# Query products of two heads as a seven-product block scheme in a two-layer decoder kernel

## The chip, the cores and the metric

The kernel runs on one core of a Trainium2 chip. The metric is the device time of one execution in microseconds (us). The kernel before took 1770.25 us, the median of three runs (1769.23 to 1772.86). Engines are named as the profile names them: PE is TensorE's matmul row and PEld its weight loads, DVE is VectorE, ACT is ScalarE, POOL is GpSimd, SP is SyncE, whose queue issues most DMAs.

## What is computed

Two decoder layers with layernorm after each of four blocks, on 4 x 256 tokens of width 512, all in float32. The change lies in the first block, a latent attention with 32 heads:

```
q_c = x @ Wq_c.T + bq_c                     # 192 wide
q   = q_c @ Wq_up.T + bq_up                 # per head 128 + 64 (rotary part)
kv  = x @ Wkv_c.T + bkv_c                   # 64 latent + 64 rotary
k   = [kv_nope @ Wk_up.T + bk_up, kv_rope]  # per head 128 + 64
v   = kv_nope @ Wv_up.T + bv_up
out = softmax(q k^T / sqrt(192)) v  ->  summed through Wo;   x = layernorm(x + out)
```

After it come a gated FFN with integer weights (1376 inner columns), a causal attention with 32 heads of 128, and a linear layer with eight low-rank experts, each followed by its layernorm.

## The kernel before, in words

**Setup (lines 101 to 189).** The weights of the first block are loaded by DMA. The key up-projection is folded into the query up-projection: for each head, a matrix `wm` of 128 + 1 columns maps the 192 + 1 compressed query rows (two pieces of 96 rows, the second with a row of ones for the bias) straight to a 128-wide query against the latent key `kT`. The 64 folded columns are computed in eight groups of four heads from `wqn` and `wkn` (line 64, copied by lines 184); the 64 rotary columns come by DMA (lines 140 to 142). `wm` is stored with the head index innermost, so one head's matrix is read with a step of 32 elements. `qcT` holds the compressed queries of all 1024 tokens, in the two pieces.

**Folded queries (lines 191 to 206).** `q_unit(h, hf)` makes the query of one head for one half of the tokens (512): two matmuls, one per piece, added up in a PSUM bank "p", then one ScalarE copy with the softmax scale. A pair of heads takes four units, eight products of 512 columns. The first pair's are made before the loop; in the loop each of the four batch steps of pair j makes one unit of pair j + 1.

**The loop (lines 297 to 318).** Sixteen head pairs j, and in each four batch steps b. A step computes the scores of its two heads (`scores0`, two banks "s"), takes row maxima on VectorE, forms the exponent's bias with `beta`, and lets ScalarE take the four exponentials with row sums. Meanwhile PE transposes the probabilities of the step before (`transposes0`, line 265, banks "t"); VectorE copies each bank to SBUF as `pT` (line 269); one query unit follows; then the output products of the step before with the latent values `cN` (`output0`, line 282, bank "o"), copied by ScalarE into `pc` (line 286). VectorE divides the new probabilities by their sums (`softmax0`, line 254). Every second pair, `value_unit` multiplies `pc` of two pairs with the value weights into `oacc` (lines 288 to 295).

**After the loop (lines 320 to 324).** For each of eight token tiles: product with `wo`, residual add (line 323), layernorm, four transposes of the new x (line 98), copy to `xT` (line 99). Then the FFN begins with the last, narrow weight chunk (`last_chunk`, line 386 on: gate in "p", up in "s"), for each token half, and with the input differences of its own seven-product scheme (line 360).

**What sets the order.** The code calls the engines in the order of the loops; the tile framework reorders each engine's instructions by its own estimate of times, and puts in the waits. PSUM has eight banks of 128 x 512 words: in this stage two each for "p", "s", "t" and "o", kept in one pool (`ps0`) that stays open through the FFN and closes behind it.

Of the kernel before, what the change touches and what calls it, by code (L numbers as in the profile page):

```python
# [9 lines left out]
F32 = mybir.dt.float32  # L10
I32 = mybir.dt.int32
AF = mybir.ActivationFunctionType
ALU = mybir.AluOpType
# [3 lines left out]
P = 128  # L17
B, S, D = 4, 256, 512
N = B * S
NT = N // P  # L20
DC = D // P
NH = 32
GH = 4
NG = NH // GH
DN, DR, DV = 128, 64, 128
RQ, RKV = 192, 64
RQ2 = RQ // 2
# [8 lines left out]
QSCALE = 1.0 / math.sqrt(DN + DR)  # L36
# [3 lines left out]
def tile_decoder2(ctx: ExitStack, tc: tile.TileContext, a: dict, out: bass.AP):  # L40
    nc = tc.nc
# [5 lines left out]
    @contextmanager  # L47
    def banks(name, **bufs):

        with tc.tile_pool(name=name, bufs=1, space=PSUM) as pool:  # L50
            ps["pool"], ps["bufs"] = pool, bufs
            yield

    def bank(tag, shape=(P, 512)):
        return ps["pool"].tile(list(shape), F32, tag=tag, name=f"ps_{tag}", bufs=ps["bufs"][tag])
# [6 lines left out]
    def mm(o, pairs):  # L62
        for i, (l, r) in enumerate(pairs):
            nc.tensor.matmul(o, l, r, start=(i == 0), stop=(i == len(pairs) - 1))  # L64
# [40 lines left out]
    NP = NH // 2  # L105
    FP = 2
    ps0 = ExitStack()
    ps0.enter_context(banks("ps0", p=2, s=2, t=2, o=2))
    with tc.tile_pool(name="l0", bufs=1) as l0, tc.tile_pool(name="l0b", bufs=2) as l0b:
        wkn = l0.tile([P, NH, RKV + 1], F32, name="wkn")  # L110

        wm = l0.tile([RQ2 + 1, 2, P + 1, NH], F32, name="wm")
# [7 lines left out]
        qcT = l0.tile([RQ2 + 1, 2, N], F32, name="qcT")  # L120
# [9 lines left out]
        for c in range(DC):  # L130
            nc.scalar.dma_start(out=wqc[:, c, :], in_=a["wqc"][:, c, :])
            nc.scalar.dma_start(out=wkvc[:, c, :], in_=a["wkvc"][:, c, :])
            for hf in range(2):
                cols = bass.ts(hf, 512)
# [16 lines left out]

        nc.vector.memset(qcT[RQ2:RQ2 + 1, 1, :], 1.0)
        outs = []
        for hf, tags in enumerate(("pst", "pst")):
            for m in range(3):
                rows_m = P if m == 2 else RQ2
                outs.append((bank(tags[m]), hf, m, rows_m))
        for c in range(DC):  # L160
            for pj, hf, m, rows_m in outs:
                lhs = wkvc[:, c, :] if m == 2 else wqc[:, c, m * RQ2:(m + 1) * RQ2]
# [3 lines left out]
        for pj, hf, m, rows_m in outs:  # L166
            cols = bass.ts(hf, 512)
# [3 lines left out]
                nc.vector.tensor_scalar(qcT[:RQ2, m, cols], pj[:RQ2], cb[:RQ2, m:m + 1], None, ALU.add)  # L171


        for g in range(NG):
            heads = slice(g * GH, (g + 1) * GH)
            for m in range(2):
                rows_m = RQ2 + m
                pj = bank("o", (P, GH, RKV + 1))
                for hh in range(GH):
                    mm(pj[:rows_m, hh, :], [  # L180
                        (wqns[g][:, hh, m * RQ2:m * RQ2 + rows_m], wkn[:, g * GH + hh, :])
                    ])
                copy = nc.scalar.copy if m == 0 else nc.vector.tensor_copy
                copy(wm[:rows_m, m, DR:, heads], pj[:rows_m].rearrange("p h c -> p c h"))

            tp = bank("t", (P, P))
            nc.tensor.transpose(tp, kT[:, bass.ts(g, P)], ident)
            nc.vector.tensor_copy(cN[:, g, :], tp[:, DR:])

        qh = {}  # L190

        def q_unit(h, hf):

            if h not in qh:
                qh[h] = l0b.tile([P, N], F32, tag=f"qh{h % 2}", name=f"qh{h}")
            cols = bass.ts(hf, 512)
            pj = bank("p")
            mm(pj, [
                (wm[:RQ2, 0, :P, h], qcT[:RQ2, 0, cols]),
                (wm[:, 1, :P, h], qcT[:, 1, cols]),  # L200
            ])
            nc.scalar.activation(qh[h][:, cols], pj, AF.Copy, scale=QSCALE)

        for u in [(h, hf) for h in range(2) for hf in range(2)]:
            q_unit(*u)

        beta = l0.tile([P, NT, NH], F32, name="beta")
        for t in range(NT):
            toks = bass.ts(t, P)
            pj = bank("p", (P, NH))  # L210
            mm(pj, [
                (qcT[:RQ2, 0, toks], wm[:RQ2, 0, P, :]),
                (qcT[:, 1, toks], wm[:, 1, P, :]),
            ])
            nc.scalar.activation(beta[:, t, :], pj, AF.Copy, scale=QSCALE)

        bvs = bv[:, 0:1]
        for n in (16, 8, 4, 2, 1):
# [3 lines left out]
        def scores0(j, b):  # L222
            keys = bass.ts(b, S)
            scs = []
            for h in (2 * j, 2 * j + 1):
                sc = bank("s", (P, 2, S))
                for qt in range(2):
                    mm(sc[:, qt, :], [(qh[h][:, bass.ts(2 * b + qt, P)], kT[:, keys])])
                scs.append(sc)
            nmx = small.tile([P, 2, 2], F32, name="nmx")  # L230
            for i, sc in enumerate(scs):
                nc.vector.tensor_reduce(nmx[:, i, :], sc, AX.X, ALU.max, negate=True)  # L232

            be = beta[:, 2 * b:2 * b + 2, 2 * j:2 * j + 2].rearrange("p t h -> p h t")
            nmb = small.tile([P, 2, 2], F32, name="nmb")
            nc.vector.tensor_tensor(nmb, nmx, be, ALU.subtract)
            bias = small.tile([P, 2, 2], F32, name="ebias")
            nc.vector.tensor_tensor(bias, nmb, be, ALU.add)  # L238
            pr = l0b.tile([P, 2, 2, S], F32, tag="pr", name="pr")
            sm = small.tile([P, 2, 2], F32, name="sm")  # L240
            for i, sc in enumerate(scs):
                for qt in range(2):
                    nc.scalar.activation(  # L243
                        pr[:, i, qt, :], sc[:, qt, :], AF.Exp, bias=bias[:, i, qt:qt + 1],
                        accum_out=sm[:, i, qt:qt + 1],
                    )
            return pr, sm
# [11 lines left out]
        def transposes0(pr):  # L259
            pTs = []  # L260
            for i in range(2):
                tp = bank("t", (P, 2, S))
                for kt in range(2):
                    for qt in range(2):
                        nc.tensor.transpose(  # L265
                            tp[:, kt, qt * P:(qt + 1) * P], pr[:, i, qt, kt * P:(kt + 1) * P], ident
                        )
                pT = l0b.tile([P, 2, S], F32, tag=f"pT{i}", name=f"pT{i}")
                nc.vector.tensor_copy(pT, tp)  # L269
                pTs.append(pT)  # L270
            return pTs

# [14 lines left out]

        def value_unit(j0, hf):
            cols = bass.ts(hf, 512)
            pj = bank("p")  # L290
            mm(pj, [(wvl[:, j, :], pc[j][:, cols]) for j in range(j0, j0 + FP)])
            if j0 == 0:
                nc.vector.tensor_scalar(oacc[:, cols], pj, bvs, None, ALU.add)
            else:
                nc.vector.tensor_tensor(oacc[:, cols], pj, oacc[:, cols], ALU.add)

        pending, flush = None, []
        for j in range(NP):
            if j == 1:
                for t in range(NT):  # L300
                    nc.gpsimd.tensor_tensor(x[:, t, :], x[:, t, :], bo, ALU.add)
            todo = [(h, hf) for h in (2 * j + 2, 2 * j + 3) for hf in range(2)] if j + 1 < NP else []
            for b in range(B):
                pr, sm = scores0(j, b)
                if pending:
                    pTs = transposes0(pending[2])
                if todo:
                    q_unit(*todo.pop(0))
                if flush and b >= 2:
                    value_unit(*flush.pop(0))  # L310
                if pending:
                    output0(pending[0], pending[1], pTs)
                pending = (j, b, softmax0(pr, sm))
            if j % FP == FP - 1:
                flush += [(j + 1 - FP, hf) for hf in range(2)]
# [2 lines left out]
            value_unit(*u)  # L318

        for t in range(NT):  # L320
            pj = bank("p")
            mm(pj, [(oacc[:, t * P:(t + 1) * P], wo0)])
            nc.vector.tensor_tensor(x[:, t, :], pj, x[:, t, :], ALU.add)
            layernorm(t)
# [14 lines left out]


    Q = 2 * P
    with tc.tile_pool(name="f0", bufs=1) as f0:
        dsc = f0.tile([P, D], F32, name="dsc")
        nc.sync.dma_start(out=dsc, in_=a["rows"][:, 1, :])
        hT = f0.tile([P, NI, N], F32, name="hT")
# [16 lines left out]
        with tc.tile_pool(name="f0i", bufs=2) as f0i, tc.tile_pool(name="f0w", bufs=3) as f0w:  # L362
# [82 lines left out]
            for c in range(NI2):  # L445
# [5 lines left out]
                for hf in range(2):  # L451
                    quarters = [slice((2 * hf + m) * Q, (2 * hf + m + 1) * Q) for m in range(2)]
                    cols = bass.ts(hf, 512)
                    up = f0w.tile([P, 2, 512], F32, tag="up", name="up", bufs=1)
                    products(lg, rights[hf], [[hT[:, 2 * c + n, q] for q in quarters] for n in range(2)])
                    for n in range(2):
                        h = hT[:, 2 * c + n, cols]
                        nc.scalar.activation(h, h, AF.Silu, scale=gsc[:, 2 * c + n:2 * c + n + 1])
                    products(lu, rights[hf], [[up[:, n, m * Q:(m + 1) * Q] for m in range(2)] for n in range(2)])
                    for n in range(2):  # L460
                        h = hT[:, 2 * c + n, cols]
# [16 lines left out]
        with tc.tile_pool(name="f0d", bufs=2) as f0d:  # L478
# [59 lines left out]
            for tt in range(NT // 2):  # L538
# [3 lines left out]
                down(tt, *now)  # L542
                for m in range(2):
                    layernorm(2 * tt + m)

    ps0.close()

# [4 lines left out]
    with banks("ps1", b0=1, b1=1, b2=1, s=2, t=2, o=1), \  # L554
# [4 lines left out]
        def xblock(k, m):  # L559
            return xT[:, 2 * k:2 * k + 2, m * HN:(m + 1) * HN]  # L560
# [6 lines left out]
        t3 = xcomb("t3", xblock(1, 1), xblock(0, 1))  # L567
        t1 = xblock(0, 1)
        nc.vector.tensor_tensor(t1, t1, xblock(0, 0), ALU.subtract)
        t2 = xcomb("t2", xblock(1, 1), t1)  # L570
        t4 = xcomb("t4", xblock(1, 0), t2)
# [214 lines left out]
        for j in range(NP):  # L786
# [15 lines left out]
            total, at, todo = sum(w for _, w in order), 0, {}  # L802
# [4 lines left out]
            for i in range(2 * B):  # L807
                h, b = 2 * j + i // B, i % B
# [5 lines left out]
                if pending:  # L814
                    pT = transposes1(pending[2])
# [18 lines left out]
    with banks("ps2", p=2, s=2, t=2, o=2), tc.tile_pool(name="f1", bufs=2) as f1:  # L834
        iscale = 1.0 / math.sqrt(DK)
        for t in range(NT):
            cols = bass.ts(t, P)
# [24 lines left out]
            tp = bank("t", (P, P))  # L862
# [91 lines left out]
```

## Time and profile before

| what | us |
|---|---|
| median of the runs | 1770.25 |
| the profiled execution | 1776.69 |
| its span | 1774.9 |
| set-up to the first folded queries | 0 to 39.0 |
| first pair's queries, beta, first scores | 39.0 to 54 |
| head-pair loop | 54 to 436 |
| residual, layernorm, first FFN matmuls | 436 to 472 |
| the rest | 472 to 1774.9 |

In the profile a group line reads: line of the kernel, engine, operation, output<-input by tile name, shapes, count | busy us, mean ns of one | idle time of the engine just before, and what ended most of it. A timeline line reads: start us, length us, engine, line, operation, and in brackets the idle time before it. An f32 matmul appears as two PE instructions, and its recorded length overlaps that of the next; what it costs is the distance from its start to the next start. A stretch line gives its bounds, its span, the busy us of PE, PEld, DVE, ACT and POOL with counts, the granted PE clock, the DMA share and GB/s.

### The profile page before, as it was taken

The numbers are of one execution on the slowest core, as the hardware profiler recorded it, in microseconds if no ns is written. First come the engines' busy times: TensorE is split into PE (matmuls) and PEld (weight loads), VectorE is DVE, ScalarE is ACT, GpSimd is POOL, SyncE is SP. The second block draws the span as 40 slices with busy tenths as digits, with TensorE's granted clock in tenths as the row PEclk, the third lists the DMA queues.
The fourth block names the chain that finished last, engine by engine and source line by source line (L and its number), as shares of the span: only waits on it lengthen the run. The fifth ranks groups of instructions, "written<-read, shape, count | busy, mean of one in ns | idle before, by whom it ended". The sixth has DMA issues, their size and how long they took to land.

```text
span 1774.9 us, 20762 instructions
## 1 busy us (share of the span) xinstructions
PE 1728.0 (97%) x7376; PEld 1206.1 (68%) x7376; DVE 1079.4 (61%) x2556; ACT 480.7 (27%) x1570; POOL 493.8 (28%) x516
## 2 busy tenths in 40 slices
PE   8999999999899998999999999999999999999988
PEld 5666666665588884767667767766776776676644
DVE  1677777767745544456656566666656665567844
ACT  1444444443222100222222222222222222222223
POOL 0200000000457335122434244234325334333220
PEclk9999999999999999999999999999999999999989
DMA  8000000000521000101001011001011010010000
GB/s 277 1 1 1 1 1 1 1 1 1 185 72 36 1 1 20 40 24 48 24 24 48 25 36 48 24 24 48 25 43 42 24 48 24 19 47 25 12 12 36
DMA packets 30985, 60.85 MB, mean 34 GB/s; under 512 B 2689, under 2 KB 20353, under 8 KB 29153
## 3 DMA queue, kind: packets, MB, share of 16 engines
q1 hardware_dynamic: 29474, 58.86, 10.6%
q8 instruction: 59, 0.97, 0.2%
q10 hardware_dynamic: 1408, 0.66, 0.1%
q14 instruction: 44, 0.36, 0.1%
HBM read 57.41 MB, written 2.10 MB: 34 GB/s over the span
## 4 chain that ended last, share of the span: by engine, by line
PE 88%; DVE 7%; DMA 2%; issue 1%; ACT 1%; POOL 1%; ACTq 0%; DVEq 0%; POOLq 0%
PE ps_b L629 20%; PE ps_s L64 12%; PE ps_b L653 11%; PE ps_p L64 10%; PE ps_b L700 9%; PE ps_o L282 4%; PE ps_t L265 3%; PE ps_o L779 3%; PE ps_s L419 3%; PE ps_t L768 2%; PE ps_o L64 2%; PE ps_o L419 2%; PE ps_p L419 2%; PE ps_o L780 2%; DVE pr L762 1%
## 5 line engine op out<-in xcount | busy, mean ns | idle before, releaser
L781 ACT COPY att<-ps_o 128x256 f32<-128x256 f32 x128 | 47.6, 372 | 521.6 <-PE ps_o L780 521.5
L243 ACT ACTIVATE pr<-ps_s,ebias 128x256 f32<-128x256 f32 x256 | 117.7, 472 | 203.0 <-DVE ebias L238 203.0
L708 DVE TENSOR_TENSOR x<-ps_b,x 128x512 f32<-128x512 f32 x180 | 122.9, 685 | 39.6 <-PE ps_b L700 29.0
L718 POOL TENSOR_TENSOR x<-x,po 128x512 f32<-128x512 f32 x90 | 112.3, 1268 | 123.4 <-DVE x L708 95.0
L752 ACT ACTIVATE pr<-ps_s,nmx 128x128 f32<-128x128 f32 (+1 forms) x256 | 105.4, 418 | 144.5 <-DVE nmx L748 144.5
L64 PE MATMUL ps_s<-kT,qh 128*128 128x256 f32 x512 | 130.8, 393 | 1.0 <-ACT pr L243 0.6
L64 PE MATMUL ps_p<-qcT,wm 96*128 96x512 f32 (+1 forms) x256 | 126.5, 618 | 0.0
L373 POOL CAST fwg<-wiwg 128x512 f32<-128x512 int32 (+1 forms) x12 | 7.4, 643 | 401.8 <-DMA wiwu<-in_wu 392.7
L762 DVE TENSOR_SCALAR pr<-pr,rc 128x128 f32<-128x128 f32 (+1 forms) x256 | 115.0, 481 | 4.3
L64 PEld LDWEIGHTS ps_s<-kT,qh 128*128 128x128 f32 x512 | 89.9, 189 | 36.3 <-ACT pr L243 20.6
L232 DVE TENSOR_REDUCE nmx<-ps_s 128x2 f32<-128x512 f32 x128 | 88.1, 688 | 37.9 <-PE ps_s L64 35.4
L64 PE MATMUL ps_s<-ck,cq 128*128 128x128 f32 (+1 forms) x512 | 106.1, 329 | 0.0
L744 DVE TENSOR_TENSOR ps_s<-ps_s,mask 128x256 f32<-128x256 f32 x128 | 55.3, 432 | 70.1 <-PE ps_s L64 66.9
L700 PE MATMUL ps_b<-ct,co 128*128 128x256 f32 x360 | 88.9, 381 | 4.0 <-POOL co L680 4.0
L269 DVE COPY pT<-ps_t 128x512 f32<-128x512 f32 x128 | 86.4, 681 | 0.0
L64 PEld LDWEIGHTS ps_p<-qcT,wm 96*128 96x128 f32 (+1 forms) x256 | 70.9, 299 | 17.6
L748 DVE TENSOR_REDUCE nmx<-ps_s 128x1 f32<-128x128 f32 (+1 forms) x256 | 79.5, 352 | 4.3
L779 PE MATMUL ps_o<-pT,v 128*128 128x256 f32 x256 | 77.3, 384 | 4.0 <-DVE pT L770 4.0
L254 DVE TENSOR_SCALAR pr<-pr,rc 128x256 f32<-128x256 f32 x256 | 79.0, 349 | 3.1
L768 PEld LDWEIGHTS ps_t<-ident,pr 128*128 128x128 f32 x384 | 50.1, 141 | 41.5 <-issue 31.6
L700 PEld LDWEIGHTS ps_b<-ct,co 128*128 128x128 f32 x360 | 67.7, 190 | 13.4 <-POOL co L680 4.2
L779 PEld LDWEIGHTS ps_o<-pT,v 128*128 128x128 f32 x256 | 47.9, 191 | 40.4 <-issue 36.5
(244 smaller groups left out, 3580.1 us busy)
## 6 DMA issues: line engine op xcount, KB each, us to landing
w_wa<-in_wq SPq DMA_DIRECT2D x16, 512.0 KB, 3.9
w_wb<-in_wk SPq DMA_DIRECT2D x16, 512.0 KB, 3.9
w_wc<-in_wv SPq DMA_DIRECT2D x8, 1024.0 KB, 4.9
w_wd<-in_wo SPq DMA_DIRECT2D x16, 512.0 KB, 3.7
wqn<-in_wqn SPq DMA_DIRECT2D x8, 386.0 KB, 13.7
wiwg<-in_wg SPq DMA_DIRECT2D x5, 512.0 KB, 3.7
wiwu<-in_wu SPq DMA_DIRECT2D x5, 512.0 KB, 3.6
wid<-in_wd SPq DMA_DIRECT2D x10, 256.0 KB, 2.6
```

The lines of the kernel that those rows point to most:

```text
L64: nc.tensor.matmul(o, l, r, start=(i == 0), stop=(i == len(pairs) - 1))
L232: nc.vector.tensor_reduce(nmx[:, i, :], sc, AX.X, ALU.max, negate=True)
L243: nc.scalar.activation(pr[:, i, qt, :], sc[:, qt, :], AF.Exp, bias=bias[:, i, qt:qt + 1], accum_out=sm[:, i, qt:qt + 1],)
L419: nc.tensor.matmul(banks_of[tag], lhs[i][:, k, :], rhs[i][:, k, :], start=first and k == 0, stop=k == 1, skip_group_check=True,)
L629: nc.tensor.matmul(acc, lhs[i][:, k, :], right[i][:, k, :], start=first and k == 0, stop=k == 1, skip_group_check=True,)
L653: nc.tensor.matmul(acc[:, tt, :], right[i][:, k, (t0 + tt) * P:(t0 + tt + 1) * P], lhs[i][:, k, :], start=first and tt == 0 and k == 0, st ...
L700: nc.tensor.matmul(st[tag][:, tt, :], lhs[i][:, (t0 + tt) * P:(t0 + tt + 1) * P], rhs[i], start=first and tt == 0, stop=True, skip_group_c ...
L708: nc.vector.tensor_tensor(xb[m][k], acc, xb[m][k], ALU.add)
L718: nc.gpsimd.tensor_tensor(xb[m][k], xb[m][k], st["p1"], ALU.add)
L752: nc.scalar.activation(pr[:, pt, :], sc[:, pt, :], AF.Exp, bias=nmx[:, qt:qt + 1], accum_out=sm[:, qt:qt + 1],)
L762: nc.vector.tensor_scalar(pr[:, pt, :], pr[:, pt, :], rc[:, qt:qt + 1], None, ALU.mult)
L779: nc.tensor.matmul(po, v[g][:, 2 * b, hv], pT[:, 0:2, :], start=True, stop=False)
```

## The change

1. **Seven block products for eight.** The two heads of a pair and the two pieces of the compressed query form a 2 x 2 block matrix on the left (`l11` to `l22`), the two pieces and the two token halves one on the right. Four sums of right blocks (`t1` to `t4`, tile `qx`) are made once by VectorE. For each pair GpSimd makes four sums of left blocks (`s1` to `s4`, tile `cw`). Seven products go to three banks "b0", "b1", "b2", each used twice: the second product of a bank is added to the first in PSUM. Between them ScalarE makes two scaled copies, and VectorE five scaled additions of a bank and an earlier result. Each batch step calls two of the seven units (the fourth calls one). So that all blocks have 97 rows, a row of zeros is added to the first piece of `qcT` and of `wm`.
2. **Banks.** In the stage: b0, b1, b2, o with one bank each, s and t with two. The folding's first half uses b2, `value_unit` b0 and b2, the `wo` products all three. `beta` is gathered in one "o" bank and copied once. `value_unit` is called in the last batch step alone.
3. **The pool** of this stage closes ahead of the FFN, which opens a new one, `psf`, with the old shares.
4. **pT of the second head** is copied by ScalarE.

```
-    ps0.enter_context(banks("ps0", p=2, s=2, t=2, o=2))
+    ps0.enter_context(banks("ps0", b0=1, b1=1, b2=1, s=2, t=2, o=1))
...
+        nc.vector.memset(qcT[RQ2:RQ2 + 1, 0, :], 0.0)
         nc.vector.memset(qcT[RQ2:RQ2 + 1, 1, :], 1.0)
+        nc.gpsimd.memset(wm[RQ2:RQ2 + 1, 0, :, :], 0.0)
...
+        qcb = [[qcT[:, k, bass.ts(hf, 512)] for hf in range(2)] for k in range(2)]
+        qx = l0.tile([RQ2 + 1, 4, 512], F32, name="qx")
+        t1, t2, t3, t4 = (qx[:, i, :] for i in range(4))
+        nc.vector.tensor_tensor(t1, qcb[0][1], qcb[0][0], ALU.subtract)
+        nc.vector.tensor_tensor(t2, qcb[1][1], t1, ALU.subtract)
+        nc.vector.tensor_tensor(t3, qcb[1][1], qcb[0][1], ALU.subtract)
+        nc.vector.tensor_tensor(t4, qcb[1][0], t2, ALU.subtract)
+        qright = (qcb[0][0], t2, qcb[1][0], t3, t1, t4, qcb[1][1])
...
-                pj = bank("o", (P, GH, RKV + 1))
+                pj = bank(("b2", "o")[m], (P, GH, RKV + 1))
...
-        def q_unit(h, hf):
-            if h not in qh:
-                qh[h] = l0b.tile([P, N], F32, tag=f"qh{h % 2}", name=f"qh{h}")
-            cols = bass.ts(hf, 512)
-            pj = bank("p")
-            mm(pj, [
-                (wm[:RQ2, 0, :P, h], qcT[:RQ2, 0, cols]),
-                (wm[:, 1, :P, h], qcT[:, 1, cols]),
-            ])
-            nc.scalar.activation(qh[h][:, cols], pj, AF.Copy, scale=QSCALE)
+        def q_units(j):
+            if j >= NP:
+                return []
+            l11, l12, l21, l22 = (wm[:, k, :P, 2 * j + n] for n in range(2) for k in range(2))
+            c = l0b.tile([RQ2 + 1, 4, P], F32, tag="cw", name="cw")
+            s1, s2, s3, s4 = (c[:, i, :] for i in range(4))
+            nc.gpsimd.tensor_tensor(s1, l21, l22, ALU.add)
+            nc.gpsimd.tensor_tensor(s2, s1, l11, ALU.subtract)
+            nc.gpsimd.tensor_tensor(s3, l11, l21, ALU.subtract)
+            nc.gpsimd.tensor_tensor(s4, l12, s2, ALU.subtract)
+            qleft = (l11, s2, l12, s3, s1, l22, s4)
+            st, o = {}, {}
+            def product(i, tag, first):
+                if first:
+                    st[tag] = bank(tag)
+                nc.tensor.matmul(st[tag], qleft[i], qright[i], start=first, stop=True, skip_group_check=True)
+                return st[tag]
+            def copy(key, acc):
+                nc.scalar.activation(o[key], acc, AF.Copy, scale=QSCALE)
+            def plus(key, acc, other):
+                nc.vector.scalar_tensor_tensor(o[key], acc, QSCALE, o[other], ALU.mult, ALU.add)
+            def first():
...
+                copy(None, product(0, "b0", True))
+            return [
+                first,
+                lambda: plus((0, 1), product(1, "b1", True), None),
+                lambda: plus((1, 1), product(4, "b2", True), None),
+                lambda: copy((0, 0), product(2, "b0", False)),
+                lambda: plus((1, 1), product(3, "b1", False), (1, 1)),
+                lambda: plus((0, 1), product(6, "b2", False), (0, 1)),
+                lambda: plus((1, 0), product(5, "b1", False), None),
+            ]
...
+        pj = bank("o", (P, NT, NH))
         for t in range(NT):
...
+            mm(pj[:, t, :], [(qcT[:, k, bass.ts(t, P)], wm[:, k, P, :]) for k in range(2)])
+        nc.scalar.activation(beta, pj, AF.Copy, scale=QSCALE)
...
-                nc.vector.tensor_copy(pT, tp)
+                (nc.scalar.copy if i else nc.vector.tensor_copy)(pT, tp)
...
-            pj = bank("p")
+            pj = bank(f"b{2 * hf}")
...
-                if todo:
-                    q_unit(*todo.pop(0))
-                if flush and b >= 2:
+                for u in todo[2 * b:2 * b + 2]:
+                    u()
+                if flush and b == B - 1:
                     value_unit(*flush.pop(0))
...
-            pj = bank("p")
+            pj = bank(f"b{t % 3}")
             mm(pj, [(oacc[:, t * P:(t + 1) * P], wo0)])
...
-    with tc.tile_pool(name="f0", bufs=1) as f0:
+    ps0.close()
+    with banks("psf", p=2, s=2, t=2, o=2), tc.tile_pool(name="f0", bufs=1) as f0:
...
-    ps0.close()
```

## The prediction

> **What bounds the kernel now.** I read the page first (busy shares, the chain that ended last), then the busy times by stretch, then the timeline inside the stage that the change touches.
>
> ```profile
> span 1774.9 us, 20762 instructions
> PE 1728.0 (97%) x7376; PEld 1206.1 (68%) x7376; DVE 1079.4 (61%) x2556; ACT 480.7 (27%) x1570; POOL 493.8 (28%) x516
> ...
> PE 88%; DVE 7%; DMA 2%; issue 1%; ACT 1%; POOL 1%; ACTq 0%; DVEq 0%; POOLq 0%
> ```
>
> TensorE is busy 97% of the span and carries 88% of the chain: work taken from it counts, if nothing else becomes late. By stretch (span, then busy us of PE, PEld, DVE, ACT, POOL):
>
> ```profile
> 106.00:155.00 49.00, 49.00 (x234) 32.98 (x234) 34.87 (x100) 21.77 (x81) 0.00 (x0) 1.00 0.00 1
> ...
> 420.00:445.00 25.00, 23.12 (x105) 12.31 (x103) 20.95 (x59) 9.10 (x33) 0.00 (x0) 1.00 0.01 2
> 445.00:475.00 30.00, 25.75 (x85) 12.36 (x86) 24.52 (x53) 6.79 (x12) 14.17 (x21) 1.00 0.71 238
> ```
>
> Two head pairs take 49 us with PE full, at full clock, and VectorE at 71%. From 420 on PE is not full: there VectorE (84%, 82%) sets the pace. Inside the loop, one step after another on PE (start, length):
>
> ```profile
> 213.70 1.99 PE L64 MATMUL ps_p<-qcT,wm 96*128 96x512 f32 x4
> ...
> 215.52 1.88 PE L64 MATMUL ps_p<-pc,wvl 128*128 128x512 f32 x4
> ...
> 217.33 1.08 PE L282 MATMUL ps_o<-pT,cN 128*64 128x256 f32 x8
> ...
> 218.35 1.99 PE L64 MATMUL ps_s<-kT,qh 128*128 128x256 f32 x8
> ...
> 220.18 1.04 PE L265 MATMUL ps_t<-ident,pr 128*128 128x128 f32 x8
> ...
> 221.05 1.99 PE L64 MATMUL ps_p<-qcT,wm 96*128 96x512 f32 x4
> ...
> 222.97 1.08 PE L282 MATMUL ps_o<-pT,cN 128*64 128x256 f32 x8
> ```
>
> Differences of starts are the slots: scores 1.83, transposes 0.87, two query products 1.82 to 1.92 (four instructions, since an f32 product is issued as two), value 1.81, output 1.02. A query product costs 0.91.
>
> **The change, part by part.**
>
> *One product fewer per pair.* 16 pairs: 15 in the loop at 0.91 and the first, in the unbroken run of eight from 39.03 to 46.02, at 6.99/8 = 0.87. Sum 14.5 us off PE.
>
> *Additions in its place.* Per pair ScalarE loses four copies of 0.61 and gains two, plus four pT copies: +1.2 us of 23.5. VectorE loses four pT copies of 0.68 and gains five scaled additions. Those stand in the second attention already, in the same form:
>
> ```profile
> L601 DVE SCALAR_TENSOR_TENSOR ck<-ps_b,p 128x512 f32<-128x512 f32 x48 | 33.2, 691 | 39.7 <-PE ps_b L629 38.7 <-PE ps_t L768 1.0
> ```
>
> ```profile
> L269 DVE COPY pT<-ps_t 128x512 f32<-128x512 f32 x128 | 86.4, 681 | 0.0
> L202 ACT ACTIVATE qh<-ps_p 128x512 f32<-128x512 f32 x64 | 38.8, 606 | 5.6 <-PE ps_p L64 5.6
> ...
> L360 POOL TENSOR_TENSOR hd<-hT 96x128 f32<-96x128 f32 x3 | 1.3, 450 | 5.3 <-DVE hT L395 5.3
> ```
>
> 5 x 0.69 - 4 x 0.68 = +0.73 us per pair: VectorE goes from about 17.4 to 18.2 of the 22.6 us that a pair will take. Not a bound in sum, but unevenly spread: in the compiled order of the changed kernel one batch step of each pair holds four of the five additions. There, from its scores' start, with 0.6 per large operation and 0.65 per addition: first maximum at 1.17, addition, second maximum to 3.0, pT copy 3.6, addition, bias 4.5, exponentials from 4.75; PE meanwhile has transposes, two products, output, a third product (6.45 in all) and is not kept waiting; VectorE ends its last scaling at about 8.1, which puts the next step's maxima 0.5 late and its pT copy at 9.95, against PE's arrival at 10.06. Cover of 0.1 only.
>
> *The pT copy on ScalarE.* Before, two products (1.9 us) stood between transposes and output; now the compiled order has one, and the other after the output. In time from the scores' start: transposes end at 2.87, ScalarE copies from 2.93 to 3.54 and is seen by PE at 3.60; the product ends at 3.61. This is level. The copy stands ahead of the same step's exponentials on ScalarE, so it isn't held by them; queued behind it are those exponentials, whose bias is ready at 3.6 (before: 4.2, since the second pT copy stood in VectorE's way), so they gain. A delay here is paid by PE directly, because the output and the next scores are behind it. For this wait and the one above I take 1.0 us over the whole loop; bounds 0 and 0.3 x 15 = 4.5. For the extra changes from output to product (three per pair, before always output to scores) 0.5, bounds 0 and 0.1 x 45 = 4.5: the product before an output shows such 0.1 (1.92 against 1.82).
>
> *Banks.* One "o" bank for two, three single "b" banks for two "p": each next writer comes 3 us or more after the reader's turn by the walk above. Nothing; without that cover it is the stalls just bounded.
>
> *Left sums on GpSimd.* Four operations of 97x128 per pair. The row nearest is 0.45 (hd, above): 1.8 us. The Trainium skill (GPSIMD Engine Reference, Performance pitfalls for Q7 kernels) speaks against it: reading with an element step over 8 bytes costs about half more, and wm is read with a step of 32 elements. By the rule 4 x 0.68 = 2.7 us per pair. No strided GpSimd row is in this trace. Both vanish behind a pair's 22.6 us, since GpSimd has 0.00 busy there and works a pair ahead; only at the start does it count.
>
> *The start.* The compiled order puts the first pair's products in among the weight folding, and its second product waits for GpSimd's sums, and these for the rotary weights:
>
> ```profile
> L141 SPq DMA_DIRECT2D wm<-in_wqr x1: 582/582/582, 13.7 to 13.7; - x1
> ...
> DMA to landing us min/median/max: 18.6/18.6/18.6
> ```
>
> They land at 32.3. Then three GpSimd operations (two first sums, then the needed one): 1.35 by the row, 2.0 by the rule, so 33.7 or 34.3. PE gets there at about 31.4 (26.48, 1.46 per group, one product) and stands 2.3 or 2.9, where before it stood 0.7 to 0.9 for folding weights at 33.17. I take the mean, 2.6, so +1.8, and against it 0.6 of a wait at 53.97 (before the second scores) that pulled-forward products now fill: +1.2. Bounds 0 and +3. The four right sums on VectorE (4 x 0.7) end near 29.3, before PE comes back to those banks; the GpSimd memset (from its 128x256 row of 0.32, an estimate of 5 us) ends before 10, and the second qcT memset likewise: nothing.
>
> *Beta.* Eight small copies become one, the matmuls stay: nothing.
>
> *The end of the loop.* In the last pair VectorE's row of operations sets a step of 5.5 us (scores at 424.64 and 430.15); without the second pT copy in front of the bias it is 5.5 - 0.55 = 4.95. But products now run ahead of their pair, so six steps instead of four lie open. Idle PE there: 4.0 before (21.6 us from 413.88 to 435.46 for 17.6 of work), about 3.6 after: -0.4.
>
> *The transition to the FFN.* The banks are closed and opened again ahead of the FFN. Before, the small last chunk's matmuls of the first token half (8 instructions each for gate and up: 6.9 us) filled PE's gaps between layernorm transposes, which wait for VectorE; so did one product (0.86). In the compiled order of the changed kernel all of these come after the last transpose.
>
> ```profile
> 463.66 0.63 PE L98 MATMUL ps_t<-ident,x 128*128 128x128 f32 x4 [0.20 <-DVE x L94]
> ...
> 465.07 3.67 PE L64 MATMUL ps_p<-xT,fwg 128*96 128x512 f32 x8 [0.78 <-DVE xT L99]
> ...
> 468.58 3.60 PE L64 MATMUL ps_s<-xT,fwu 128*96 128x512 f32 x8
> ...
> 472.02 1.03 PE L419 MATMUL ps_p<-xT,fwg 128*128 128x256 f32 x4
> ```
>
> Before, from the first residual add (436.69) to the last transpose is 27.0, to the products 35.3, or 34.5 when the one already done is credited. After: VectorE is freed in this stretch of one pT copy (0.6), one xT copy that now follows (0.6) and three input differences (2.1): its 26.8 to the last scaling become 23.5, and 0.3 for a bank wait: 23.8. Then 0.6 for the transpose and 4 x 3.48 for all four runs: 38.3. That is +3.8, less 0.3 of small stalls at 473 to 475 that fall away: +3.5. Bounds +1.5 (VectorE quicker) and +6. From there on all orders are the same.
>
> **Sum.** -14.5 + 1.0 + 0.5 + 1.2 - 0.4 + 3.5 = -8.7 us. The profiled execution took 1776.69 (span 1774.9 and 1.8 around it), so 1768.0 there; the median of the runs is 1770.25, 0.36% lower, so **1761.5** by their measure.
>
> **The rivals.** A difference within 0.2% (3.5 us) is about what measurement can't tell from none.
> 1. *As forecast*: a gain of 5 to 11 us. For: PE full in the loop, cover found for each wait. 1761.5, own range 1759 to 1765.
> 2. *The covers hold fully*: no stalls in the loop, start at 0, transition +1.5: -14.5 - 0.4 + 1.5 = -13.4, 1757. For: steps in the second attention use this scheme with PE full. Against: the transition is read off the order and VectorE's load.
> 3. *Small waits in each pair*: output waits for pT by 0.3 and out-to-product exposes 0.1 thrice: +9 in place of 1.5, so -1.2, 1769. For: covers of 0.0 and 0.1.
> 4. *VectorE sets the loop's pace* (other side): in the step with four additions the backlog isn't worked off, and each pair stalls. The point of decision is 8.7/16 = 0.55 us per pair over what I counted; at 0.9 per pair it is +5.7, 1776. For: 6.3 of 6.45 us in that step are VectorE's. Against: the steps after it have 1.5 us slack each.
>
> That the scheme doesn't take effect is excluded: the compiled order has seven products per pair.
>
> **How the numbers follow.** Chances: 0.52, 0.18, 0.18, 0.12. Faster by over 0.2% (under 1766.7): nearly all of 1, all of 2, a third of 3: 0.75. Within: the rest of 1 and most of 3: 0.13. Slower (over 1773.8): most of 4 and the edge of 3: 0.12. Eight in ten: from 1756 (rival 2's end) to 1770 (rival 3).
>
> **What would show it.** Right: a pair of pairs repeats every 47 us with PE full; output instructions show no idle behind ps_t or pT; all last-chunk matmuls follow the last transpose and the first FFN product comes 38 us after the first residual add; a PE idle of 2 to 3 us near 32. Wrong: PE idle before L324 put down to ACT pT or DVE pT, or before the scores; a repeat over 48 us.

## The result, and where the time is after

The change took 1774.80 us, the median of 20 runs (1770.53 to 1777.48), against 1772.09 us for the kernel before in 20 runs (1769.23 to 1775.62). The ratio is 1.0012, with a 95% interval of 1.0004 to 1.0019: 2.7 us slower, a small difference but clear of none by its interval, where a gain of 8.7 (1761.5) was forecast. So 11.4 us of the expected gain are missing.

First the page of the changed kernel (span, busy times, shares of the chain that ended last), and then its busy times by stretch (PE, PEld, DVE, ACT, POOL, then the granted clock, the DMA share and GB/s):

```profile
span 1774.1 us, 20868 instructions
PE 1716.7 (97%) x7344; PEld 1190.7 (67%) x7344; DVE 1111.1 (63%) x2577; ACT 499.3 (28%) x1593; POOL 529.8 (30%) x581
...
PE 87%; DVE 8%; issue 1%; POOL 1%; ACT 1%; DMA 1%; SPq 0%; ACTq 0%; DVEq 0%; POOLq 0%
```

```profile
46.00:50.00 4.00, 4.00 (x21) 3.23 (x21) 0.45 (x1) 0.00 (x0) 0.00 (x0) 0.66 0.00 0
50.00:54.00 4.00, 4.00 (x10) 2.53 (x9) 1.46 (x3) 0.38 (x1) 3.31 (x6) 0.50 0.00 0
54.00:58.00 4.00, 4.00 (x8) 2.23 (x8) 1.28 (x2) 0.60 (x1) 4.00 (x4) 0.56 0.00 0
58.00:62.00 4.00, 2.05 (x5) 0.78 (x3) 3.90 (x2) 0.00 (x0) 4.00 (x4) 1.00 0.00 0
...
106.00:153.00 47.00, 46.66 (x229) 30.30 (x228) 37.78 (x101) 24.36 (x85) 4.10 (x8) 1.00 0.00 1
...
420.00:445.00 25.00, 20.63 (x94) 11.28 (x92) 22.18 (x63) 8.89 (x31) 2.25 (x6) 1.00 0.18 51
445.00:475.00 30.00, 23.09 (x65) 11.42 (x66) 17.71 (x35) 3.63 (x7) 11.37 (x16) 0.77 0.58 196
```

Inside the loop the change did what it promised: the same instruction, the copy of `pc` in a pair's first step, comes at 141.23 and again two pairs later, at 188.29. That is 47.06 us; before, the same two copies came at 132.70 and 181.59, which is 48.89. The difference of 1.83 is two products of 0.91. The changed kernel's two lines, and behind them the two of the kernel before:

```profile
141.23 0.38 ACT L328 COPY pc<-ps_o 128x256 f32<-128x256 f32 x1
...
188.29 0.38 ACT L328 COPY pc<-ps_o 128x256 f32<-128x256 f32 x1
```

```profile
132.70 0.39 ACT L286 COPY pc<-ps_o 128x256 f32<-128x256 f32 x1
...
181.59 0.39 ACT L286 COPY pc<-ps_o 128x256 f32<-128x256 f32 x1
```

Outside the loop two places differ. From 46 to 58 PE is busy, but at half to two thirds of its clock, and from 58 to 62 it stands for half of the time. From 445 to 475 it is granted 0.77 of its clock, where before it had 1.00.

Following that one copy through both kernels shows when the time was lost. In the first step of the first pair (pair 0) the changed kernel is 10.7 us behind (71.35 for 60.67), with two more query products behind it (14, before 12), so 8.9 for equal work. Over the next two pairs it gains nothing, since its products run ahead; from pair 3 on it gains 1.83 per two pairs, is 0.4 ahead at the first step of pair 14 and 7.1 ahead at the last step (434.86 for 441.98). It loses that again before the FFN's first product (472.29 for 472.02). So there are two losses: one before 71 us, one between the loop and the FFN.

**The first place.** Timeline of the changed kernel around 50 us (start, length, engine; in brackets the idle time ahead of it and what ended it):

```profile
44.83 3.77 PE L64 MATMUL ps_o<-wm,qcT 97*128 97x32 f32 x28
...
48.41 2.06 PE L223 MATMUL ps_b<-qcT,cw 97*128 97x512 f32 x2
50.26 1.92 PE L223 MATMUL ps_b<-qx,wm 97*128 97x512 f32 x2
...
50.62 0.62 POOL L212 TENSOR_TENSOR cw<-wm 97x128 f32<-97x128 f32 x1 [11.88 <-PE ps_b L223]
...
52.62 9.81 POOL L343 TENSOR_TENSOR x<-x,bo 128x512 f32<-128x512 f32 x8
...
58.13 4.32 DVE L278 TENSOR_TENSOR nmb<-nmx,beta 128x4 f32<-128x4 f32 x1
...
62.97 0.15 DVE L280 TENSOR_TENSOR ebias<-nmb,beta 128x4 f32<-128x4 f32 x1
...
63.20 1.10 PE L223 MATMUL ps_b<-qx,cw 97*128 97x512 f32 x2 [3.15 <-DVE ebias L280]
```

The same additions in the kernel before:

```profile
44.22 9.85 POOL L301 TENSOR_TENSOR x<-x,bo 128x512 f32<-128x512 f32 x8 [4.15 <-DMA bo<-in_rows]
```

Two things are to be seen. The eight additions `x + bo` on GpSimd started at 44.22 before; now the framework has put them behind the weight sums of pair 2 (in the code they stand ahead of them), which wait (11.88 us) until PE has let go of pair 0's sums, whose buffer they reuse. They run from 52.62 to 62.43. The subtraction `nmb`, which takes 0.15 us elsewhere (median of 64), takes 4.32 and ends when that row ends. Behind it stand the exponent's bias, the exponentials, and with them the score banks that PE needs. And a product takes 1.85 here (48.41 to 50.26), twice its 0.91, behind the row of 28 narrow `beta` products (32 columns each) that begins at 44.83.

**The second place.** PE around the end of the layernorms, in the changed kernel:

```profile
450.49 1.09 PE L98 MATMUL ps_t<-ident,x 128*128 128x128 f32 x4 [3.07 <-DVE mv L87]
453.64 2.22 PE L98 MATMUL ps_t<-ident,x 128*128 128x128 f32 x8 [2.06 <-DVE ve L89]
456.74 5.41 PE L64 MATMUL ps_p<-xT,fwg 128*96 128x512 f32 x8 [0.88 <-DVE xT L99]
461.99 3.60 PE L64 MATMUL ps_s<-xT,fwu 128*96 128x512 f32 x8
465.42 3.60 PE L64 MATMUL ps_p<-xT,fwg 128*96 128x512 f32 x8
468.86 3.60 PE L64 MATMUL ps_s<-xT,fwu 128*96 128x512 f32 x8
472.29 1.02 PE L462 MATMUL ps_p<-xT,fwg 128*128 128x256 f32 x4
```

PE has nothing but four transposes at a time and waits 2 to 3 us for each group. Four transposes then take 1.09 where they took 0.63, and the first run of the last chunk takes 5.25 us (456.74 to 461.99) where the next take 3.43.

### The profile page after: what moved, and what is told of

It is laid out like the page before. It is cut to its first block, busy times and chain, and to the rows that moved or that the text cites. A ratio compares the mean times of both kernels' runs of the same rounds, so it can differ in the third digit from the quotient of the medians.

```text
span 1774.1 us, 20868 instructions
## 1 busy us (share of the span) xinstructions
PE 1716.7 (97%) x7344; PEld 1190.7 (67%) x7344; DVE 1111.1 (63%) x2577; ACT 499.3 (28%) x1593; POOL 529.8 (30%) x581
## 4 chain that ended last, share of the span: by engine, by line
PE 87%; DVE 8%; issue 1%; POOL 1%; ACT 1%; DMA 1%; SPq 0%; ACTq 0%; DVEq 0%; POOLq 0%
PE ps_b L670 20%; PE ps_b L694 11%; PE ps_s L64 11%; PE ps_b L741 10%; PE ps_b L223 6%; PE ps_o L324 3%; PE ps_o L820 3%; PE ps_s L462 3%; PE ps_t L307 2%; PE ps_b L64 2%; PE ps_o L64 2%; PE ps_p L64 2%; PE ps_t L809 2%; PE ps_o L462 2%; PE ps_p L462 2%; PE ps_o L821 2%
## 5 line engine op out<-in xcount | busy, mean ns | idle before, releaser
L822 ACT COPY att<-ps_o 128x256 f32<-128x256 f32 x128 | 47.6, 372 | 520.5 <-PE ps_o L821 520.4
L64 PE MATMUL ps_s<-kT,qh 128*128 128x256 f32 x512 | 125.8, 388 | 0.5
L64 PEld LDWEIGHTS ps_s<-kT,qh 128*128 128x128 f32 x512 | 98.1, 194 | 40.7 <-issue 24.4
L285 ACT ACTIVATE pr<-ps_s,ebias 128x256 f32<-128x256 f32 x256 | 117.7, 472 | 18.7 <-DVE ebias L280 16.4
L212 POOL TENSOR_TENSOR cw<-wm 97x128 f32<-97x128 f32 x16 | 10.0, 628 | 267.3 <-PE ps_b L223 249.2
L296 DVE TENSOR_SCALAR pr<-pr,rc 128x256 f32<-128x256 f32 x256 | 83.4, 368 | 4.3
L311 ACT COPY pT<-ps_t 128x512 f32<-128x512 f32 x64 | 37.4, 585 | 158.6 <-PE ps_t L307 158.6
L801 DVE RECIPROCAL rc<-sm 128x2 f32<-128x2 f32 x128 | 20.8, 162 | 86.7 <-ACT pr L793 86.5
L324 PE MATMUL ps_o<-pT,cN 128*64 128x256 f32 x512 | 70.0, 391 | 3.6 <-ACT pT L311 1.5
```

What stands on the lines that cost most here:

```text
L285: nc.scalar.activation(pr[:, i, qt, :], sc[:, qt, :], AF.Exp, bias=bias[:, i, qt:qt + 1], accum_out=sm[:, i, qt:qt + 1],)
L324: nc.tensor.matmul(po[i * RKV:(i + 1) * RKV, :], cN[:, 2 * b + kt, :], pTs[i][:, kt, :], start=(kt == 0), stop=(kt == 1),)
```

## The experiments

The theory was that these two places hold all that is missing: GpSimd's row with the low clock at the start, and the closed pool at the transition. Rival A was that waits in the loop eat the gain, rival B that the clock falls for reasons of its own. All runs below are medians; the kernel before, run beside them, took 1772.24 us beside the first four, 1772.29 beside the next four and 1770.22 beside the last two.

**Beta by tile.**

```
-        pj = bank("o", (P, NT, NH))
         for t in range(NT):
-            mm(pj[:, t, :], [...])
-        nc.scalar.activation(beta, pj, AF.Copy, scale=QSCALE)
+            pj = bank("o", (P, NH))
+            mm(pj, [...])
+            nc.scalar.activation(beta[:, t, :], pj, AF.Copy, scale=QSCALE)
```

> Edit: the changed kernel, but beta is again multiplied and copied tile by tile (eight copies), so that its 32 narrow products can no longer run as one block of 3.8 us. Theory (start): this block, whose instructions stream 32 columns each, makes the clock fall to half from 48 to 58 us; without it PEclk stays 1.00 from 44 to 58, the five query products there take 0.9 us each and not 1.85, and scores are ready about 5 us earlier. But GpSimd's eight additions x+bo still run back to back from about 50 and still hold up the first small VectorE subtraction (4.3 us before), so most of the 5 us is given back to that wait: 1 to 3 us less than the changed kernel, 1772 to 1774. Rival A (the loop lost the time): no change, 1774.8, clock or not. Rival B (the low clock comes from elsewhere, such as the pause at 32 us, and merely falls there): PEclk is low in the same place again.

Measured: 1773.09 (ratio 1.0006, 0.9999 to 1.0012), 1.7 less than the changed kernel. VectorE and GpSimd in its timeline:

```profile
49.60 9.83 POOL L343 TENSOR_TENSOR x<-x,bo 128x512 f32<-128x512 f32 x8
...
52.16 7.29 DVE L278 TENSOR_TENSOR nmb<-nmx,beta 128x4 f32<-128x4 f32 x1
```

The clock stays at 1.00 up to 54 us, `nmb` is ready 6 us earlier, and takes 7.29 us in place of 4.32. It ends with GpSimd's row again. While PE waits for it, the clock falls after all, to 66 us, which was not expected:

```profile
54.00:58.00 4.00, 0.14 (x1) 0.00 (x0) 4.00 (x1) 0.00 (x0) 4.00 (x4) 0.67 0.00 0
58.00:62.00 4.00, 1.61 (x5) 1.35 (x6) 3.00 (x6) 2.08 (x10) 1.43 (x2) 0.50 0.00 0
```

So this edit moves the low clock more than it removes it, and is worth little because a longer wait is behind it.

**`x + bo` spread out.** One addition per pair, held in program order behind that pair's weight sums:

```
-            if j == 1:
-                for t in range(NT):
-                    nc.gpsimd.tensor_tensor(x[:, t, :], x[:, t, :], bo, ALU.add)
             todo = q_units(j + 1)
+            if 1 <= j <= NT:
+                tc.keep_in_program_order(nc.gpsimd.tensor_tensor(x[:, j - 1, :], x[:, j - 1, :], bo, ALU.add))
```

> Edit: the changed kernel, but GpSimd's eight additions x+bo stand one after each pair's weight sums (pairs 1 to 8) in place of eight in a row. Theory (start): the first small VectorE subtraction with two operands in SBUF took 4.32 us because it waited for GpSimd to end its row of eight; with a single addition at 51 to 52 it takes 0.15, the exponentials start at about 58.8 and not 63.2, and PE's idle of 3.15 us at 60 and the second stretch of low clock (63 to 68) go. The low clock from 48 to 58 stays. 4 to 6 us less than the changed kernel: 1769 to 1771. In the loop an addition of 1.23 us may stretch one small VectorE operation per pair; at most 0.3 us for each of eight pairs. Rival A (loop): no change, 1774.8.

Measured: 1766.45 (ratio 0.9969, 0.9956 to 0.9983), 8.35 less than the changed kernel, more than the 4 to 6 expected. Its timeline:

```profile
50.13 1.27 POOL L343 TENSOR_TENSOR x<-x,bo 128x512 f32<-128x512 f32 x1
...
52.27 0.17 DVE L278 TENSOR_TENSOR nmb<-nmx,beta 128x4 f32<-128x4 f32 x1
```

The subtraction takes 0.17 and PE has no idle from 42 to 62. The estimate had taken the wait as 4.3 us; where the clock does not fall first it is 7.3 to 7.7. Rival A falls: no product, bank or scaled addition of the loop was changed, and 8 us came back.

**One set of banks for attention and FFN.** `fbank` takes b0 and b1 in turn for "p" and b2 and o for "o"; the lines after it are numbered eight higher.

```
-    ps0.close()
-    with banks("psf", p=2, s=2, t=2, o=2), tc.tile_pool(name="f0", bufs=1) as f0:
+    with tc.tile_pool(name="f0", bufs=1) as f0:
...
-                pg = bank("p")
+                pg = fbank("p")
...
-                        banks_of[tag] = bank(tag, (P, Q))
+                        banks_of[tag] = fbank(tag, (P, Q))
```

> Edit: the changed kernel, but the eight banks are not closed and opened again ahead of the FFN: the FFN takes its p tiles in turn from b0 and b1 and its o tiles from b2 and o. Theory (transition): the last chunk's products go back between the layernorm transposes, PE is not left idle from 440 to 456, the clock stays at 1.00 there (0.50 from 447 to 460 before), and the first FFN product comes 35 us after the first residual addition in place of 39.5: 4 to 5 us less than the changed kernel, 1770 to 1771. Rival (VectorE sets this stretch whatever PE does): less than 1.5 us.

Measured: 1766.22 (ratio 0.9969, 0.9959 to 0.9979), 8.6 less than the changed kernel, where 4 to 5 were expected; in the profiled execution 1.5 of it lies ahead of the transition, where the clock fell later. The last chunk lies between the transposes again, and the FFN's first product comes 26.3 us after the first residual addition (428.72 to 454.98) in place of 42.1, with the last chunk's second half still to follow:

```profile
446.04 3.94 PE L72 MATMUL ps_b<-xT,fwg 128*96 128x512 f32 x6 [0.34 <-DVE xT L107]
449.82 0.60 PE L106 MATMUL ps_t<-ident,x 128*128 128x128 f32 x4
...
454.98 1.03 PE L469 MATMUL ps_b<-xT,fwg 128*128 128x256 f32 x4
```

The clock is not at 1.00 throughout, as was expected, but it is low for a shorter time: 0.66 from 445 to 450 and 1.00 from there on, where the changed kernel has 0.67, 0.50 and 0.50 from 445 to 460. `nmb` shows the other loss in full here, 7.69 us.

**All three edits.**

> Edit: the three edits before this one together (beta by tile, x+bo spread over eight pairs, one set of banks for attention and FFN). Theory: nothing holds the start up any more, so the clock's 5 us and the wait's 5 to 6 us both come back, and the transition's 4 to 5: 14 to 16 us less than the changed kernel, about 1759 to 1761, and 11 to 13 less than the kernel before. If the three are one cause (a low clock that follows from any idle of PE), the sum is less than that of the parts; if the loop lost the time, it is still near 1770.

Measured: 1755.46 (1754.23 to 1755.83; ratio 0.9907, 0.9893 to 0.9921): 19.3 less than the changed kernel, where 14 to 16 were expected, and 16.8 less than before. The parts are 1.7, 8.35 and 8.6, so 18.7: they add up, and this version beats both kernels.

**The clock's part by itself: `x + bo` spread and beta by tile, pools closed.**

> Edit: x+bo spread over pairs 1 to 8 and beta by tile, the pools closed as in the changed kernel. The executions of the kernel with x+bo spread alone lie in two groups, six from 1762 to 1764.5 and six from 1768.5 to 1772. Theory: the second group is the one in which the clock falls to half after the block of 32 narrow beta products; with beta by tile that block is gone and all lie near 1763, so the median falls by 2 to 4 us. Rival: the two groups come from the transition to the FFN, where PE stands idle; then they stay, and the median is 1766 again.

Measured: 1762.94 (1762.39 to 1764.59; ratio 0.9950, 0.9938 to 0.9963), 3.5 less than with the spread alone, and none of five executions in the upper group. Once GpSimd's row is out of the way, taking the block of narrow products apart is worth 3.5 us by the medians.

That the two groups of the spread version are executions with and without the fall is likely, but not shown: none of the upper group was traced; on record is their mean clock over the whole execution, 0.985 to 0.987 for 0.987 to 0.989 in the lower group. Over the traces of all kernels, the clock fell within the block in three of the five that have it, and between 10 and 55 us in none of the seven without it. And rival B holds in part: between 550 and 625 us, where these three run the same code, the mean clock was 0.95 in the kernel before, 0.98 in the changed kernel and 1.00 in this version. So an execution can differ by up to some 4 us for this alone (an estimate, 0.05 of 75 us), and 3.5 us from five executions is a rough figure.

**The kernel before, with beta in one block.**

> Edit: the kernel before, with beta's 32 products in one bank and one copy, as the change has them; all else as before. In the compiled order they form one unbroken row of 4 us ahead of the first scores. Theory: the clock falls to half after it in some executions: 1 to 4 us more than before, 1773 to 1776. Rival: the block does nothing by itself, since GpSimd's x+bo ends ahead of the first subtraction here: within 1 us of before.

Measured: 1779.25 (ratio 1.0043, 1.0030 to 1.0055), 7.0 more than before. The clock did fall (0.83 from 46 to 50 and 0.75 from 50 to 54), but at the loop's first copy of `pc` that had cost only 0.4 us. The rest, 6.8, came over the next eight steps, 0.86 in each, in which the compiled order had changed: query products were split, and output products with them. PE in such a step:

```profile
83.48 1.13 PE L64 MATMUL ps_p<-qcT,wm 97*128 97x512 f32 x2
84.54 0.65 PE L282 MATMUL ps_o<-pT,cN 128*64 128x256 f32 x2
85.12 1.23 PE L64 MATMUL ps_p<-qcT,wm 96*128 96x512 f32 x2
86.28 1.08 PE L282 MATMUL ps_o<-pT,cN 128*64 128x256 f32 x6
```

Two of the eight output instructions take 0.58 and the other six 1.01, where all eight took 1.02; such a step lasts 6.6 us and not 5.76, with PE shown as full. So this run does not isolate the clock; it is inconclusive on what it was made for.

**GpSimd's row kept, but early.** Pair 2's weight sums are held behind `x + bo`:

```
+            pin = tc.keep_in_program_order if j == 2 else (lambda ins: ins)
-            nc.gpsimd.tensor_tensor(s1, l21, l22, ALU.add)
+            pin(nc.gpsimd.tensor_tensor(s1, l21, l22, ALU.add))
...
```

> Edit: the changed kernel, but GpSimd's row of eight x+bo is held ahead of the weight sums of pair 2, so that it starts when x and bo have landed (about 43 to 44) and not when PE has released pair 0's sums (50 to 52). Theory: what costs is where the row lies, not that it is a row: it ends at 53 to 54, the first small subtraction (ready at 52.3) waits 1 to 2 us in place of 4.3 to 7.7, and most of the gain of the spread version is there: 1765 to 1768. Rival (the row itself costs, wherever it lies, because VectorE has other operations with two operands in SBUF): within 2 us of the changed kernel.

Measured: 1767.78 (1764.51 to 1769.72; ratio 0.9972, 0.9961 to 0.9984), 7.0 less than the changed kernel. Its row ran from 42.95 to 52.8 and `nmb`, at 57.77, took 0.16. It is the place of the row that costs, not that it is a row. The clock fell here too, within the block of narrow products, with PE busy throughout. That costs some 4.9 us: the copy of `pc` in pair 2's first step comes at 112.35, in the profile of the spread version, where the clock held, at 107.47. Timeline and stretches:

```profile
42.95 9.85 POOL L344 TENSOR_TENSOR x<-x,bo 128x512 f32<-128x512 f32 x8 [4.15 <-DMA bo<-in_rows]
...
44.78 3.47 PE L64 MATMUL ps_o<-wm,qcT 97*128 97x32 f32 x28
...
48.06 2.05 PE L224 MATMUL ps_b<-qcT,cw 97*128 97x512 f32 x2
49.90 1.92 PE L224 MATMUL ps_b<-qx,wm 97*128 97x512 f32 x2
...
57.77 0.16 DVE L279 TENSOR_TENSOR nmb<-nmx,beta 128x4 f32<-128x4 f32 x1
```

```profile
46.00:50.00 4.00, 4.00 (x21) 2.97 (x21) 0.40 (x1) 0.00 (x0) 4.00 (x4) 0.70 0.00 0
50.00:54.00 4.00, 4.00 (x10) 2.44 (x9) 1.82 (x3) 0.39 (x1) 3.92 (x6) 0.50 0.00 0
54.00:58.00 4.00, 4.00 (x8) 2.33 (x7) 1.11 (x3) 0.60 (x1) 0.81 (x2) 0.52 0.00 0
```

**The kernel before, with nothing but the banks closed and opened.**

```
+    ps0.close()
-    with tc.tile_pool(name="f0", bufs=1) as f0:
+    with banks("psf", p=2, s=2, t=2, o=2), tc.tile_pool(name="f0", bufs=1) as f0:
...
-    ps0.close()
```

> Edit: the kernel before, but its banks are closed and opened again, with the same tags, ahead of the FFN; nothing else. In the compiled order all four runs of the last chunk then follow the last layernorm transpose. Theory: this alone is the price of the transition, 6 to 9 us more than before (PE idle between transposes, half clock for the last chunk): 1778 to 1781. Rival (the price comes with the new sharing of banks in the residual and value products): less than 2 us.

Measured: 1779.67 (ratio 1.0048, 1.0034 to 1.0061), 7.4 more than before. From the first residual addition (435.81) to the FFN's first product (477.83) it takes 42.0 us, as in the changed kernel (430.22 to 472.29, 42.1), where the kernel before took 35.3. The two lines of the edit carry the whole price of the transition. PE there:

```profile
456.17 1.06 PE L98 MATMUL ps_t<-ident,x 128*128 128x128 f32 x4 [2.28 <-DVE mv L87]
458.59 2.23 PE L98 MATMUL ps_t<-ident,x 128*128 128x128 f32 x8 [1.35 <-DVE ve L89]
461.69 6.00 PE L64 MATMUL ps_p<-xT,fwg 128*96 128x512 f32 x8 [0.87 <-DVE xT L99]
467.53 3.60 PE L64 MATMUL ps_s<-xT,fwu 128*96 128x512 f32 x8
```

**All three edits, both pT copies on VectorE again.**

> Edit: the version with all three edits (1755.5), but both pT copies on VectorE as before the change. Theory (the prediction's walk through the loop was right that VectorE's cover is thin): VectorE goes from 37.7 to about 43 us of the 47 that two pairs take, and in the step with four scaled additions it has 7.0 us of work for 6.5 of PE's, so a pair loses about 0.5 us, and the last steps without products are 0.55 us longer each: 5 to 12 us more, 1761 to 1767. Rival (the copy's place doesn't matter, the cover is wide): less than 2 us.

Measured: 1788.92 (ratio 1.0101, 1.0084 to 1.0117), 33 more than with the copy on ScalarE: two pairs take about 51 us in place of 47.06. The direction was right and the size far off. VectorE is busy 40.6 of 49 us; but here, too, the compiled order splits output products around a query product, so how much of the 33 is VectorE and how much the order was not told apart.

**All three edits, the row of eight early.**

> Edit: the version with all three edits, but x+bo as a row of eight ahead of pair 2's weight sums (43 to 53 us) in place of one per pair. Theory: with full clock the first small subtraction is ready at about 52, the row ends at 53 to 54, so 0 to 2 us are lost there; in the loop eight stretched VectorE operations of 1.2 us go, which PE's cover hid anyway: 1755 to 1757. Rival (single additions in the loop cost something each): 1 to 3 us less than 1755.5.

Measured: 1757.14 (1754.17 to 1759.32; ratio 0.9918, 0.9903 to 0.9932). It can't be told from the spread version (0.9907): in the steady loop a single addition per pair costs nothing that shows.

## Why the prediction was wrong, step by step

- *One product fewer, 14.5.* Right: 1.83 us per two pairs.
- *Waits in the loop, 1.0 + 0.5.* Next to nothing: the repeat fell by the whole two products. From 72 to 405 us the changed kernel's trace has six waits of PE, 1.2 us in all (the engine's line, what it waited for, us, times, longest):

```profile
PE ps_o L324 <- DVE nmb L278: 1.2, 6, 0.2
```

  Whether the cover hung on the ScalarE copy is not shown: the reverse cost 33 us, but with another order of products as well. The fourth rival, VectorE as the loop's pace, did not come to pass; that the time landed near its 1776 is chance. A pair was given 22.6 us, which takes about two products off 24.5 and not one; 23.5 was measured (47.06 / 2), and nothing hangs on it.
- *Left sums on GpSimd.* Their length is right: 0.63, 0.44, 0.56 and 0.52 (means), 2.15 per pair, between 1.8 by the nearest row and 2.7 by the rule for strided reads: a fifth more than the nearest row, not half. What failed is "both vanish behind a pair's 22.6 us, since GpSimd has 0.00 busy there ... only at the start does it count", and with it *the start, +1.2, bounds 0 and +3*. The working asked who waits for the sums of the first pair. It did not ask what stands behind the sums of the third in GpSimd's queue: the row `x + bo`, moved from 44 to 52 us and onto `nmb`. That is 8.35 us, outside the bounds.
- *The start's own terms.* They were too dear, which hid part of the miss. PE stood 0.20 for the first sums, not 2.6: the rotary weights landed at 30.9 (issued at 14.0, 16.9 to landing) and not at 32.3, and PE came at 32.6 and not at 31.4. In the version with all three edits the first copy of `pc` comes 0.4 later than before (61.04 for 60.67), although two more products (1.8 us) are done: the start is 1.4 better there, where +1.2 was forecast.
- *Beta, "nothing".* With eight copies the 32 narrow instructions came in groups of 4, 8, 8 and 12, with scores in between. With one copy 28 of them follow each other, for 3.05 us where the clock holds (43.82 to 46.87 in the spread version) and 3.58 where it falls (44.83 to 48.41 in the changed kernel). By the medians this is 3.5 us once the row is gone, hidden behind the row before that.
- *The end of the loop, -0.4.* Right. The steps became 4.95 us, as forecast (the copies of `pc` in the last pair come at 420.00, 424.95, 429.90 and 434.86). From the first copy to the last the kernel before takes 381.31 us, the version with all three edits 364.44, so 16.9 less. In between it has 18 query products fewer (98 for 116), 16.4 us at 0.91; 0.5 is left for the loop's end and waits together.
- *The transition, +3.5.* The order was read rightly, the size was not: 42.1 us from the first residual addition to the FFN's first product, where 38.3 was worked out. The last scaling ends 24.4 after that addition (23.8 forecast), the transposes take 1.1 and not 0.6, the wait for the last xT copy (0.9) was left out, and the last chunk takes 15.55 and not 13.9. Two of the four are the half clock. 7.5 us by the runs, above the bound of 6.

So the steps that failed are three: GpSimd's queue behind the sums of the third pair (put at nothing), `beta` (put at nothing), and the size of the transition.

By the runs, the way from the changed kernel to the version with all three edits is 1774.80 to 1766.45 (row spread, 8.35), to 1762.94 (beta by tile, 3.5), to 1755.46 (one set of banks, 7.5), and that version is 16.8 below before: 14.5 for the products and 2.3 more, of which the traces put 1.4 at the start and 0.5 at the loop. That these steps add up to the +2.7 that was measured follows from how they were taken and proves nothing further. The row is shown by two edits of its place, the pool by an edit in each direction; how far the 3.5 of `beta` is the clock stays open, as said above. The forecast for the work that was removed was right; the three places outside it took all of it back.

## What to carry to other kernels

When an engine that was idle is given new work, list what it does later, and ask whether the new work can hold that up: a queue in order turns one wait for a buffer into a delay for all behind it. Price a stretch by PE's granted clock as well as its busy time, above all where narrow products are gathered into one row or PE works in short bursts between waits. Here, closing a pool kept all that came after it behind the last use of its banks, so what had been interleaved across its end came after it.

## What the runs showed of the hardware

- A VectorE subtraction of 128x4 with both inputs in SBUF took 4.32, 7.29 and 7.69 us beside GpSimd's row of eight additions, and 0.15 to 0.17 without it. The Trainium skill (SBUF — State Buffer, Who interferes with whom) says that such a VectorE instruction contends with a GpSimd instruction that reads SBUF, and, of VectorE's modes with two ports, that whoever comes second is blocked for the whole instruction. The traces agree that it is blocked, but not on the length: one GpSimd instruction is 1.23 us, and the wait ran over three to six of their ends to the end of the row. In the kernel before, two such operations got in at the next end (0.66 and 1.19 us). What decides between the two was not found.
- The clock fell to half while PE was busy without a gap, 2.5 to 3.3 us into a row of products of 32 columns: the row begins at 44.83 in the changed kernel, at 44.78 with GpSimd's row early and at 45.31 in the kernel before with `beta` in one block, and by the granted clock of each us the fall is at 47.3, 47.6 and 48.6. The skill (TensorE: Matmul & The Clock Gate, What's actually happening) tells of half clock after a window of some 3.4 us without activity. Here no window was without instructions, so having instructions in progress did not keep the clock up. With the same row of products the clock held at 1.00 in the profiles of the spread version and of the one with one set of banks. What decides it was not found.
- Eight output instructions into 64 columns each take 1.02 us one after another, and 0.58 + 1.01 when a query product is put in after the second. PE shows as full in both cases.
